# Making keys and values of four batches of the second cross-attention during the first experts' sorting

## The chip, the cores and the metric

One core of one Trainium2 chip runs the whole program. The metric is the device time of one execution in microseconds (us). Every operand is float32. The engines are TensorE (PE in the profile, with PEld for its weight loads), VectorE (DVE), ScalarE (ACT), GpSimd (POOL) and SyncE (SP), which here only issues transfers.

## The reference

A decoder of two layers on 16 sequences of 112 tokens of width 256, with a context of 16 x 375 x 256 that both layers read. Cut to what matters:

```
x = x + L0_attn(layernorm(x))                 # linear attention, 16 heads
x = x + L0_xattn(layernorm(x), ctx, ctx)      # softmax, 16 heads of 16
n = layernorm(x)
s = sigmoid(n @ gate_w + gate_b)              # 16 experts, the best two per token
x = x + n + shared_mlp(n) + sum(w_k * expert_k(n))
x = x + L1_attn(layernorm(x))                 # softmax, 16 heads of 64
x = x + L1_xattn(layernorm(x), ctx):          # softmax, 8 heads of 64
      cn = layernorm(ctx) * g2 + b2           # with a norm inside
      k, v = split(cn @ Wkv)                  # 256 -> 512 and 512
x = x + L1_ffn(layernorm(x))                  # 8 experts of width 1024, capacity 33 per sequence
```

K and V of the second cross-attention depend on the context and on weights alone, not on x.

## The kernel before, in words

The program keeps x in SBUF as 112 x 16 x 256 and works stage by stage. All large weights go through one SBUF tensor, `w_all`, of 3 x 6144 columns; `load_w` (line 155 on) loads a weight into a part of it through SP's queue.

The first cross-attention (from line 632, closures `scores`, `shifted`, `weights`, `values`) runs 16 batches of four quads of heads. The order of TensorE, VectorE, GpSimd and SP is written out by hand there. While batch b is worked on, K and V of batch b+1 are made (`prep_c`, `prep_k`, `prep_v`), spread over partitions by eight small transfers each (`kz<-kn`, `qz<-qn`), and the weights of expert b are loaded. `ctx_stats` takes mean and variance of each context for the later stage. After the loop come the last batch's division, transposes, projection, norm and router logits, and between them on TensorE the shared expert of the first expert stage in four groups of four batches: `shared_up` (line 765: eight PE instructions of 448 columns), `swiglu` (line 346: Silu on ScalarE, a product on VectorE), `shared_down` (line 774: eight PE instructions and two additions to x on VectorE).

The first expert stage (from line 888) orders only TensorE by hand; a scheduler orders the other engines by its own estimate of durations. It takes the sigmoid, the best two experts of each token (`top_two`, line 284), counts tokens before each by matmuls with `both` and `cnt`, and makes slot numbers `su` for both choices. 32 indirect transfers on GpSimd's queue (line 963, `xg<-xrow,su`) scatter the rows of x with two more columns (row number and weight, `xrow<-meta`, line 982) into the DRAM buffer `xg`, which was filled with zero rows early on (line 343). The rows are read back in 43 blocks of 128 (`fetch`, line 991, `xb<-xg`); every fetch waits for all scatters. The fetches run five blocks ahead through eight buffers:

```
for n in range(NB0 + 3):
    if n < NB0:
        fetch(n + 5)
        turn(n)          # two transposes (996), copy to bxT on VectorE (998)
    if 0 <= n - 1 < NB0:
        up(n - 1)        # four PE instructions with the block's expert
    if 0 <= n - 2 < NB0:
        turn_act(n - 2)
    if 0 <= n - 3:
        down(n - 3)      # own and to on VectorE (1025, 1026), scatter to yo
```

`own` and `to` are the target rows of a block's result, made from the columns of xb alone. The three W_qkv weights of the next stage (one MB each) are loaded ahead of the fetches.

The self-attention of the second layer (`pieces1`, `scores1`, `turned1`, `values1`) runs 32 units of one batch and half of the heads. Each unit takes three small pieces from a list `todo` that makes the following q, k and v; at the list's end stand `x1_first`, the pieces of the next stage for batch 0.

The second cross-attention (closures from line 1241) runs 32 units (b, u) of one batch and four heads. A unit issues the transposes of its softmax weights (line 1319), the scores of the next unit (1287), then fill work, then its values (1335). The fill work for batch b+1 is: `c_piece` (normalise the context, lines 234 and 1256, with scale and bias on ScalarE, 1259), four `k_piece` (1266 copies on ScalarE) and three `v_piece` (1273 copies on VectorE). When b+1 is a multiple of 4, four `q_piece` for the next four batches come in the first unit too. The softmax goes VectorE maximum (1298), ScalarE exponential (1299), VectorE reciprocal (1308), GpSimd division (1310). The second experts follow. A matmul in float32 shows as two PE instructions.

Of the kernel before, what the change touches and what calls it, by code (L numbers as in the profile page):

```python
# [18 lines left out]
S = 375  # L19
# [75 lines left out]
def tile_decoder(ctx: ExitStack, tc: tile.TileContext, t: dict, out: bass.AP):  # L95
# [238 lines left out]
    lg = f0.tile([L, B, E0], F32, tag="lg", name="lg")  # L334
    fill = f0.tile([128, RW], F32, tag="fill", name="fill")
    xg = dr.tile([NB0 * BLK, RW], F32, tag="xg", name="xg")
# [10 lines left out]
    def swiglu(sp, pg, pu, n):  # L347
# [3 lines left out]
        return sg  # L351

    cstack = ExitStack()
    cxp = pool(cstack, "cx", 2)
    cxs = {b: load_ctx(cxp, b) for b in range(2)}


# [284 lines left out]
    with ExitStack() as ph:  # L642
# [3 lines left out]
        def ctx_stats(b):  # L646
            cx = cxs.pop(b)
            for j in range(NKC):
                stats_of(cmv[:, b * NKC + j, :], cx[:, j, :])
            rstd_pow(cr[:, b * NKC : (b + 1) * NKC], cmv[:, b * NKC : (b + 1) * NKC, 1])  # L650
            if b + 2 < B:
                cxs[b + 2] = load_ctx(cxp, b + 2)


# [109 lines left out]

        def shared_up(g):
            pg, pu = bank(), bank()
            for i, p in enumerate((pg, pu)):
                mm_sum(
                    p[:, : 4 * L],
                    [(w_sh[:, i * 256 + c * 128 : i * 256 + (c + 1) * 128], xT(c, 4 * g, 4)) for c in range(2)],  # L770
                )
            return swiglu(lp, pg[:, : 4 * L], pu[:, : 4 * L], 4 * L)

        def shared_down(g, act):
            for j in range(2):
                po = bank()
                for i in range(2):
                    a = (2 * j + i) * L
                    mm(po[:L, i * D : (i + 1) * D], act[:, a : a + L], w_sh[:, 512:], start=True, stop=True)
                b = 4 * g + 2 * j  # L780
                xb = x[:, b : b + 2, :].rearrange("p b d -> p (b d)")
                nc.vector.tensor_add(xb, xb, po[:L, :])

        def out0(b):
# [11 lines left out]
        with tc.manual_schedule(engines={E.PE, E.DVE, E.Pool, E.SP}):  # L796
# [21 lines left out]
            for n, (b, g) in enumerate(quads):  # L818

                if b + 1 < B and g == 0:  # L820
                    prep_c(b + 1)
                    prep_q(b + 1)
                if b + 1 < B and g == 1:
                    prep_k(b + 1)
                if b + 1 < B and g == 2:
                    prep_v(b + 1)
                if g == 3:
                    load_expert(b)
                if g == 1 and b > 1:
                    norm_T(b - 2)  # L830
                if g == 3 and b + 2 < B:
                    norm_T(b + 2)
                if b:
                    if g == 2 and b > 1:
                        logits(b - 2)
                    if g == 1:
                        divide(b - 1)
                    if g == 2:
                        oT[b - 1] = out_T(b - 1)
                    if g == 3:  # L840
                        out_proj(b - 1, oT.pop(b - 1))
                qm = shifted(b, g)
                if n + 1 < len(quads):
                    scores(*quads[n + 1])

                if g == 0:
                    if b + 2 < B:
                        stats(b + 2)
                    if b > 1:
                        out_norm(b - 2)  # L850
                if g == 1 and b + 2 < B:
                    norm(b + 2)
                if g == 2 and b + 1 < B:
                    ctx_stats(b + 1)
                if g == 3 and b:
                    stats(b - 1)
                pr = weights(b, g, qm)
                if behind is not None:
                    values(*behind)
                behind = (b, g, pr)  # L860
            out_norm(B - 2)
            a0 = shared_up(0)
            values(*behind)
            norm_T(B - 2)
            a1 = shared_up(1)
            divide(B - 1)
            shared_down(0, a0)
            logits(B - 2)
            oT = out_T(B - 1)
            a2 = shared_up(2)  # L870
            out_proj(B - 1, oT)
            stats(B - 1)
            shared_down(1, a1)
            out_norm(B - 1)
            norm_T(B - 1)
            shared_down(2, a2)
            logits(B - 1)
            a3 = shared_up(3)
            shared_down(3, a3)

    e0s.close()
    cstack.close()
    with tc.issue_after(kz_loaded[B - 1]):
        w_qkv = load_w(2 * WR, [t["L1_attn_W_qkv"][i] for i in range(3)])

# [4 lines left out]
    with ExitStack() as ph:  # L890
        lp = pool(ph, "f0", 2)
        l1 = pool(ph, "f0one", 1)
        one = lambda shape, name: l1.tile(shape, F32, tag=name, name=name)
        with tc.manual_schedule(engines={mybir.EngineType.PE}):
            lgf = lg.rearrange("p b n -> p (b n)")
# [6 lines left out]
            both = one([L, B * E0], "both")  # L902
            nc.vector.tensor_add(both, flat(oh0), flat(oh1))

            pc = bank()
            for i in range(2):
                mm(pc[:, i * L : (i + 1) * L], both[:, i * 128 : (i + 1) * 128], ones[:L, :L], start=True, stop=True)
            cnt = one([128, 2, L], "cnt")
            nc.vector.tensor_copy(cnt.rearrange("p i l -> p (i l)"), pc[:, : 2 * L])
            pr = bank()  # L910
            later = const("later").rearrange("p (i n) -> p i n", i=2)
# [4 lines left out]
            pn = bank()  # L916
            mm_sum(pn[:L, :E0], [(cnt[:, i, :], const("same")) for i in range(2)])

            nt = one([L, E0, NT // BLK], "nt")
# [15 lines left out]
            for k, o in enumerate((oh0, oh1)):  # L935
# [4 lines left out]
                slots.append(su)  # L940

            tot = one([L, B], "tot")
            meta = one([L, 2, B, 2], "meta")
            nc.vector.tensor_add(tot, v0, v1)
            nc.vector.reciprocal(tot, tot)
            nc.vector.tensor_copy(meta[:, :, :, 0], const("row_id", L).rearrange("p (k b) -> p k b", k=2))
            for k, v in enumerate((v0, v1)):
                nc.vector.tensor_mul(meta[:, k, :, 1], v, tot)

# [29 lines left out]

            for k in range(2):  # L980
                for g in range(4):
                    nc.vector.tensor_copy(xrow[:, 4 * g : 4 * g + 4, D:], meta[:, k, 4 * g : 4 * g + 4, :])
                    for b in range(4 * g, 4 * g + 4):
                        scatter("xg", xg, slots[k][:, b : b + 1], xrow[:, b, :])

            xbs, xTs, cols, acts, aTs = {}, {}, {}, {}, {}

            def fetch(j):
                if j < NB0:
                    xbs[j] = lp.tile([BLK, RW], F32, tag="xb", name="xb", bufs=8)  # L990
                    after_all("xg", nc.sync.dma_start(xbs[j], xg[j * BLK : (j + 1) * BLK, :]))

# [23 lines left out]
            def down(j):  # L1016
# [10 lines left out]
                scatter("yo", yo, to[:, 0:1], os_[:, :])  # L1027

            for j in range(5):
                fetch(j)  # L1030
            for n in range(NB0 + 3):
# [7 lines left out]
                if 0 <= n - 3:  # L1039
                    down(n - 3)  # L1040
    f0s.close()
    cxp = pool(cstack, "cx", 2)
# [90 lines left out]
    with ExitStack() as ph:  # L1133
# [108 lines left out]

        def fetch(b):
            if b < B:
                cxs[b] = load_ctx(cxp, b)

        def c_piece(b, c):
            if c == 0:
                fetch(b + 2)
                for j in range(NKC):  # L1250
# [103 lines left out]
        def combine(b):  # L1354
# [8 lines left out]
        x1_first = (  # L1363
            [lambda c=c: c_piece(0, c) for c in range(2)]
            + [lambda m=m: q_piece(0, m) for m in range(4)]
            + [lambda m=m: k_piece(0, m) for m in range(4)]
            + [lambda j=j: v_piece(0, j) for j in range(3)]
        )
        with tc.manual_schedule(engines={mybir.EngineType.PE}):
# [51 lines left out]
            for n, (b, u) in enumerate(units):  # L1421
                pT = turned(pr)
                pr = scores(*units[n + 1]) if n + 1 < len(units) else None
                if u == 0:
                    nc.gpsimd.tensor_add(x[:, b, :], x[:, b, :], bout)
                if b + 1 < B:
                    if u == 0:
                        c_piece(b + 1, 0)
                        c_piece(b + 1, 1)
                if late:  # L1430
# [5 lines left out]
                if u == 0 and b:  # L1436
                    project(oT2.pop(b - 1), wo, 4, b - 1, keep=(mv1, r1))
                if b + 1 < B:
                    if u == 0:
                        if (b + 1) % 4 == 0:  # L1440
                            q_piece((b + 1) // 4, 0)
                            q_piece((b + 1) // 4, 1)
                        k_piece(b + 1, 0)
                        k_piece(b + 1, 1)
                        if (b + 1) % 4 == 0:
                            q_piece((b + 1) // 4, 2)
                            q_piece((b + 1) // 4, 3)
                        v_piece(b + 1, 0)
# [139 lines left out]
```

## Time and profile before

| What | us |
|---|---|
| median of 3 runs | 1801.3 (1796.4 to 1809.83) |
| the profiled execution | 1802.55 |
| its span, first to last instruction | 1800.8 |
| TensorE busy | 1607.3 (89%) |
| VectorE, ScalarE, GpSimd busy | 973.5, 604.5, 518.3 |
| chain that ended last, TensorE's share | 55% |
| last matmul of the routing ends | 503.2 |
| first transposes of an expert block | 551.72 |
| first scores of the second cross-attention | 985.59 |
| last unit's transposes of that stage end | 1358.6 |

The times of single instructions come from the timeline of the profiled execution, counted from the span's start. In such a row stand start, duration, engine, line and operation, output and inputs, shape and count, and in brackets how long the engine had been idle and what released it. L116 is the helper that all matmul sums go through, so there the tile names tell the work. In the rows of the slices each digit is a tenth of a slice of 45 us.

### The profile page before, as it was taken

To read this page: it belongs to the slowest core of one execution; us is meant where nothing else is said; L and a number is where in the kernel's file an instruction comes from. 1 tells how busy PE (TensorE), PEld (TensorE's weight loads), DVE (VectorE), ACT (ScalarE), POOL (GpSimd) and SP (SyncE) were. 2 spreads that over 40 slices of the span, in tenths; PEclk is the share of its full clock that TensorE was granted. 3 is DMA by queue.
4 is the path that set the end of the run, shared out by engine and by line. 5 is a ranking of instruction groups with operands and counts; after the bars stand their busy time and mean duration, and the time that the engine had idled before them with its cause. 6 is when DMAs were issued, how large, how long until landed. Compare 5 with 4: busy or idle time off the path is not lost.

```text
span 1800.8 us, 30940 instructions
## 1 busy us (share of the span) xinstructions
PE 1607.3 (89%) x11755; PEld 1207.5 (67%) x11755; DVE 973.5 (54%) x2635; ACT 604.5 (34%) x1456; POOL 518.3 (29%) x685
## 2 busy tenths in 40 slices
PE   7889999999806968999999999999997999979992
PEld 5766666666504746788786566666665888858881
DVE  7976777777623437777665545655456222232222
ACT  3433444444302522233323333444341333313330
POOL 6641221211153523333332444434441000030003
PEclk9999999999958979999999999999997999989996
DMA  6402222222224451000000100000001444454422
GB/s 173 107 9 52 59 72 65 60 64 56 71 80 124 145 194 52 2 1 1 1 1 9 41 18 18 19 12 19 15 16 33 146 137 147 160 158 153 152 83 67
DMA packets 96077, 125.57 MB, mean 70 GB/s; under 512 B 14353, under 2 KB 81082, under 8 KB 95930
## 3 DMA queue, kind: packets, MB, share of 16 engines
q1 hardware_dynamic: 88042, 107.98, 19.8%
q0 software_dynamic: 5184, 13.13, 2.3%
q10 hardware_dynamic: 2704, 2.49, 0.5%
q8 instruction: 94, 1.54, 0.4%
q14 instruction: 53, 0.43, 0.1%
HBM read 94.40 MB, written 21.18 MB: 64 GB/s over the span
## 4 chain that ended last, share of the span: by engine, by line
PE 55%; DMA 3%; DVE 3%; POOL 2%; issue 1%; ACT 1%; POOLq 0%; ACTq 0%; DVEq 0%; SPq 0%
PE pT L116 41%; PE pT L1319 3%; PE pT L1287 2%; PE pT L1335 2%; DMA got<-eo,row 2%; PE pT L1194 1%; PE pT L1229 1%; PE pT L1215 1%; PE pT L1120 1%; DMA yb<-yo 1%; POOL pr L1310 1%; PE pT L1514 1%; PE pT L263 1%; PE pT L1256 1%; DVE x_res L1359 0%
## 5 line engine op out<-in xcount | busy, mean ns | idle before, releaser
L1310 POOL TENSOR_SCALAR pr<-pr,den 112x375 f32<-112x375 f32 x128 | 155.9, 1236 | 197.0 <-DVE den L1308 197.0
L1490 DVE SCALAR_TENSOR_TENSOR hT<-pT,vT,gt 128x264 f32<-128x264 f32 x128 | 62.9, 492 | 241.8 <-ACT gt L1489 241.7
L116 PE MATMUL pT<-xnT,w_all 128*128 128x224 f32 (+2 forms) x736 | 161.6, 371 | 0.5 <-DVE xnT L265 0.5
L116 PEld LDWEIGHTS pT<-xnT,w_all 128*128 128x128 f32 x736 | 132.5, 195 | 17.5 <-issue 13.9
L1527 POOL DMA_INDIRECT got<-eo,row x32 | 30.1, 942 | 394.0 <-DVE hT L1490 215.6
L712 ACT ACTIVATE pr<-pT 125x336 f32<-125x336 f32 x256 | 94.6, 456 | 133.8 <-PE pT L703 133.8
L116 PE MATMUL pT<-w_all 128*128 128x264 f32 (+1 forms) x576 | 136.7, 394 | 0.6 <-ACT w_all L596 0.6
L116 PE MATMUL pT<-cT,w_all 128*128 128x375 f32 x384 | 134.3, 489 | 0.2 <-ACT cT L1259 0.2
L116 PE MATMUL pT<-w_all,cT 128*125 128x256 f32 (+1 forms) x384 | 133.3, 490 | 0.0
L687 DVE TENSOR_REDUCE mx<-pT 112x1 f32<-112x375 f32 x256 | 122.1, 539 | 11.9 <-PE pT L685 10.5
L116 PE MATMUL pT<-hT,w_all 128*128 128x264 f32 x512 | 119.4, 392 | 6.6 <-ACT hT L1495 6.6
L116 PEld LDWEIGHTS pT<-w_all 128*128 128x128 f32 (+1 forms) x576 | 110.3, 193 | 20.3 <-ACT w_all L596 0.8
L116 PE MATMUL pT<-e1T,w_all 128*128 128x264 f32 x512 | 118.4, 390 | 0.0
L1207 POOL TENSOR_TENSOR pr<-pr,den 112x448 f32<-112x448 f32 x64 | 59.2, 946 | 200.6 <-DVE den L1205 149.4
L116 PEld LDWEIGHTS pT<-hT,w_all 128*128 128x128 f32 x512 | 99.0, 194 | 24.4 <-ACT hT L1495 7.0
L116 PEld LDWEIGHTS pT<-e1T,w_all 128*128 128x128 f32 x512 | 97.9, 193 | 16.7
L116 PE MATMUL pT<-w_all,oT 128*112 128x256 f32 x448 | 106.4, 383 | 0.1
L116 PEld LDWEIGHTS pT<-cT,w_all 128*128 128x128 f32 x384 | 71.5, 192 | 52.2 <-issue 10.1
L116 PE MATMUL pT<-w_all,xnT 128*112 128x256 f32 (+1 forms) x320 | 104.7, 475 | 1.8 <-DMA w_all<-in_L_attn_Wv_dram 0.9
L1489 ACT ACTIVATE gt<-pT,vT 128x264 f32<-128x264 f32 x128 | 61.3, 480 | 114.6 <-PE pT L116 91.1
L116 PEld LDWEIGHTS pT<-w_all,cT 128*125 128x125 f32 x384 | 69.5, 187 | 43.6 <-issue 31.5
L1144 ACT COPY pT<-pT 112x448 f32<-112x448 f32 (+1 forms) x64 | 34.1, 532 | 168.0 <-PE pT L1319 90.2
(248 smaller groups left out, 2986.9 us busy)
## 6 DMA issues: line engine op xcount, KB each, us to landing
w_all<-in_L_ffn_w_c_fc_dram SPq DMA_DIRECT2D x16, 1024.0 KB
w_all<-in_L_ffn_w_gate_dram SPq DMA_DIRECT2D x16, 1024.0 KB
w_all<-in_L_ffn_w_c_proj_dram SPq DMA_DIRECT2D x16, 1024.0 KB
cx<-in_ctx_dram SPq DMA_DIRECT2D x32, 375.0 KB
kz<-kn SPq DMA_DIRECT2D x128, 46.9 KB
xg<-fill SPq DMA_DIRECT2D x1, 5547.0 KB
xb<-xg SPq DMA_DIRECT2D x43, 129.0 KB
eo<-os SPq DMA_DIRECT2D x16, 264.0 KB
```

Source lines behind the costliest of these rows:

```text
L116: mm(o, l, r, start=(i == 0), stop=(i == len(terms) - 1))
L687: nc.vector.tensor_reduce(mx[b % 2][:, g, i, 16:17], ps[i][:L, :S], AX.X, ALU.max, negate=True)
L712: nc.scalar.activation(pr[:, i, :], pw[i][:KC, : NKC * L], AF.Exp)
L1144: nc.scalar.copy(dst, src)
L1207: nc.gpsimd.tensor_tensor(pr[:, k], pr[:, k], bcast(den[:, k, :], L), ALU.mult)
L1287: mm(ps[2 * s + k][:L, :S], qTs[b // 4][rows(k), m, (b % 4) * L : (b % 4 + 1) * L], kTs[b][rows(k), m, :], start=True, stop=True,)
L1310: nc.gpsimd.tensor_scalar(pr[:, n, :], pr[:, n, :], den[:, n : n + 1], None, ALU.mult)
L1319: nc.tensor.transpose(pt[:KC, (n % 4) * L : (n % 4 + 1) * L], pr[:, i, j * KC : (j + 1) * KC], ident[:L, :L])
L1335: mm(po[rows(k), s * L : (s + 1) * L], vs[b][:, j, h * 64 : (h + 1) * 64], pT[:, 3 * (2 * s + k) + j, :], start=(j == 0), stop=(j == NKC - 1),
L1489: nc.scalar.activation(gt, ps[1][:, :HS], AF.Identity, bias=vec(n_v + e * NJ + j), scale=1.0)
L1490: nc.vector.scalar_tensor_tensor(hT[:, j, :], ps[0][:, :HS], vec(12 + e * NJ + j), gt, ALU.add, ALU.mult)
L1527: nc.gpsimd.indirect_dma_start(out=got[:, :], out_offset=None, in_=eo[b // HB][:, :], in_offset=bass.IndirectOffsetOnAxis(ap=row[k][:, b : ...
```

## The change

- `AHEAD = (0, 4, 8, 12)`: for these batches the contexts are loaded once more at the end of the first cross-attention (`ctx_ahead`), normalised on VectorE (`norm_ahead`), transposed and scaled (`c_ahead`), and K and V are made (`k_ahead`, `v_ahead`, copied by ScalarE). Each K and each V is stored to DRAM (`kd`, `vd`, 0.77 MB each) from ScalarE's queue. These are 36 pieces in a list `ahead`: for each batch two c, four k, three v. `take(n)` issues the next n on TensorE: seven in the tail of the first cross-attention, eight before the count of tokens, one inside it, 13 after the first 16 scatters are issued, seven at the end.
- The shared expert moves from that tail to beside the last 16 scatters: group g-1 after the scatters of group g.
- The scheduler no longer orders VectorE between the sigmoid and the end of `take(7)`: that part is in the order of the program. The blocks' VectorE work (bxT, own, to) stays with the scheduler. The row number and weight columns (`told`) and the first slots `su` come in another order.
- Wkv of the second cross-attention is loaded a first time in batch 2 of the first cross-attention. The three W_qkv loads move from ahead of the fetches to behind fetches 12, 17 and 22.
- In the second cross-attention no c, k and v pieces are made for batches 0, 4, 8, 12; `k_load` and `v_load` bring them from DRAM on SP's queue. The four q pieces are spread two and two over the pair of units.
- The zero rows for `xg` are copied from a part of `w_all` in place of a tile of their own.

```diff
+    def norm_ahead(i):
+        for j in range(NKC):
+            n = AHEAD[i] * NKC + j
+            normed(acxs[i][:, j, :], acxs[i][:, j, :], cmv[:, n, 0:1], cr[:, n : n + 1])
...
+    def k_ahead(i, m):
...
+        pk = bank()
+        mm_sum(pk[:, :S], [(wkv_a[0][:, c, m * 128 : (m + 1) * 128], acTs[i][:, c, :]) for c in range(2)])
+        nc.scalar.copy(akv[i][:, m, :], pk[:, :S])
+        if m == 3:
+            nc.scalar.dma_start(kd[AHEAD[i]], akv[i])
...
+                if (b, g) == (2, 0):
+                    wkv_a += load_w(2 * WR, [t["L1_xattn_Wkv"]])
...
+                if b == B - 1 and g in (1, 2):
+                    norm_ahead(g - 1)
...
             out_norm(B - 2)
-            a0 = shared_up(0)
+            take(3)
             values(*behind)
             norm_T(B - 2)
-            a1 = shared_up(1)
+            take(1)
             divide(B - 1)
-            shared_down(0, a0)
             logits(B - 2)
+            take(1)
             oT = out_T(B - 1)
-            a2 = shared_up(2)
+            take(1)
             out_proj(B - 1, oT)
             stats(B - 1)
-            shared_down(1, a1)
+            take(1)
             out_norm(B - 1)
             norm_T(B - 1)
-            shared_down(2, a2)
             logits(B - 1)
-            a3 = shared_up(3)
-            shared_down(3, a3)
...
-        with tc.manual_schedule(engines={mybir.EngineType.PE}):
+        with tc.manual_schedule(engines={mybir.EngineType.PE, mybir.EngineType.DVE}):
...
+            take(8)
...
+            norm_ahead(2)
...
+            take(1)
...
+            norm_ahead(3)
+            for g in range(4):
+                told(0, g)
...
+            for g in range(4):
+                rows_to(0, g)
+            take(len(ahead) - 7)
+            for g in range(4):
+                told(1, g)
+                rows_to(1, g)
+                if g:
+                    shared(g - 1)
+            shared(3)
+            take(7)
+
+        with tc.manual_schedule(engines={mybir.EngineType.PE}):
...
+                    i = (j - 12) // 5
+                    if j in (12, 17, 22):
+                        with tc.issue_after(got.ins):
+                            w_qkv.extend(load_w(2 * WR + 2048 * i, [t["L1_attn_W_qkv"][i]]))
...
+        def k_load(b):
+            kTs[b] = lp.tile([128, 4, S], F32, tag="qk", name="kt")
+            nc.sync.dma_start(kTs[b], kd[b])
...
-            [lambda c=c: c_piece(0, c) for c in range(2)]
-            + [lambda m=m: q_piece(0, m) for m in range(4)]
-            + [lambda m=m: k_piece(0, m) for m in range(4)]
-            + [lambda j=j: v_piece(0, j) for j in range(3)]
+            [lambda m=m: q_piece(0, m) for m in range(4)]
+            + [lambda: k_load(0), lambda: v_load(0)]
...
+                if b + 1 in AHEAD and u == 0:
+                    k_load(b + 1)
+                    v_load(b + 1)
```

## What was predicted

> **What bounds the kernel now.** I read the busy slices first, then the windows around the hole that they show, then the timelines of that hole and of the second cross-attention.
>
> ```profile
> ## 2 busy tenths in 40 slices
> PE   7889999999806968999999999999997999979992
> POOL 6641221211153523333332444434441000030003
> PEclk9999999999958979999999999999997999989996
> 500.00:520.00 20.00, 3.19 (x11) 2.25 (x9) 6.40 (x19) 0.00 (x0) 9.34 (x10) 0.59 0.17 51
> 520.00:540.00 20.00, 0.00 (x0) 0.00 (x0) 0.34 (x2) 0.00 (x0) 15.13 (x17) 0.50 0.30 93
> ```
>
> A slice is 45 us. TensorE is nearly full everywhere but in slice 11 (495 to 540 us). The windows (columns: PE, PEld, DVE, ACT, POOL busy, granted clock, DMA share, GB/s) say who works there: only GpSimd, and the clock is at half.
>
> ```profile
> 500.72 2.47 PE L116 MATMUL pT<-call,cnt 128*112 128x256 f32 x8
> 551.72 1.19 PE L996 MATMUL pT<-call,xb 128*128 128x128 f32 x4 [48.54 <-DMA xb<-xg]
> 507.92 1.20 POOL L963 DMA_INDIRECT xg<-xrow,su  x1 [23.10 <-DVE su L939]
> 546.80 0.94 POOL L963 DMA_INDIRECT xg<-xrow,su  x1 [0.30 <-issue]
> 549.52 3.66 SPq L991 DMA_DIRECT2D xb<-xg  x8
> 553.71 0.15 DVE L1025 TENSOR_SCALAR own<-xb 128x1 f32<-128x1 f32 x1 [0.27 <-DMA xb<-xg]
> ```
>
> 32 scatters at 1.247 us each (507.92 to 547.7) hold TensorE for 48.5 us; the blocks' rows xb come only after the last. Elsewhere TensorE is the bound:
>
> ```profile
> 1064.60 1.52 PE L1287 MATMUL pT<-kt,qt 64*112 64x375 f32 x8
> 1071.87 2.69 PE L116 MATMUL pT<-cT,w_all 128*128 128x375 f32 x8
> 1077.40 1.88 PE L116 MATMUL pT<-w_all,cT 128*125 128x512 f32 x4
> 1349.93 1.52 PE L1287 MATMUL pT<-kt,qt 64*112 64x375 f32 x8
> 1357.99 0.58 PE L1319 MATMUL pT<-call,pr 112*125 112x112 f32 x3 [0.63 <-POOL pr L1310]
> ```
>
> 1064 is a unit (four heads of one batch) with K and V of the next batch in it; no wait is marked. 1349.93 is the last unit, with nothing to fill it: from its scores to the end of its transposes it takes 1357.99 + 0.58 - 1349.93 = 8.64 us, however little TensorE does, because the softmax passes through VectorE, ScalarE and four GpSimd divisions of 1236 ns. That is the floor of a unit.
>
> **Second cross-attention, batches 4, 8, 12: gain.** The pair of units before such a batch (its K, V and the four q pieces in it) takes 1064.60 to 1092.56 = 27.96 us. From the PE timeline, by starts: its first unit is 17.40 us, less context transposes 0.69, K 2.53, V 1.81, and two of four q pieces 3.00 = 9.37. The second is 10.55, less V 3.45 and K 2.62, plus the two q pieces 3.00 = 7.48, so the floor of 8.64 holds. Pair after: 18.0; gain 9.95, times three = **29.9 us**. Of the 11.1 us of work removed per pair 1.15 goes to the floor. K and V come back by two loads of 0.77 MB on SP's queue. They may start once the buffers of batch b-2 are free, a whole pair (over 22 us) before the scores that need them; at the 124 GB/s of the first xb fetches and contexts before (1.8 MB between 549.52 and 563.9) both take 12.7 us. Cost 0, covered by that pair; behind them on SP wait only context loads of later batches.
>
> **End of the self-attention, batch 0: gain.** There 11 us of context, K and V pieces sit among the last three units (957.66 to 984.67). Rebuilt with what stays: values at 962.4, last scores 963.3, two transposes and the last q piece until 967.5. The softmax of the last scores took 8.5 us in the unit before (955.68 to 964.14, where the transposes after GpSimd start), so TensorE waits until 971 to 972, then transposes, out-projection 3.5, values 0.9: first cross scores at 976.7 instead of 985.59, gain 8.9. The 3.4 us wait may drop the clock; up to 3 us, I charge 1. **7.9 us.**
>
> **From the end of the first cross-attention to the expert blocks: loss.** Order of instructions in the built kernel, costed by rows:
> - VectorE normalises two contexts inside the last batch: 6 at 0.41 us, between the maxima and the next query, on the chain there: 1.8 us later.
> - The shared expert's 20.5 us of matmuls (four times 3.2 and 1.9) leave the tail; seven small pieces (1.3 to 1.8 us each) take their place. Chain of the last batch (divide, transposes, projection, statistics, norm, logits) rebuilt row by row: last logits at 483.9 instead of 486.7; sigmoid 2.6; 12 routing operations at 0.455 without the 3.5 us that VectorE spent waiting for the shared expert: `both` at 492.1 against 498.76. Eight more pieces (10 us) keep TensorE until 493.7; the three routing products then run at full clock with one V piece (1.8) between; slots 3.5 us after them; first scatter 502.0 against 507.9. Normalising contexts 8 and 12 (2.4 us) lies beside these matmuls.
> - Scatters are 32 as before: first xb load at 502.0 + 41.6 = **543.6** against 549.5.
> - TensorE meanwhile: 13 pieces 16.1 us, shared expert groups 6.4 us each; up-matmuls of group 3 end near 536. And there it stops: in VectorE's stream the scheduler put own and to of blocks 0 to 3 ahead of group 3's gate product. They wait for rows fetched after all scatters: 553.71 + 0.15 - 549.52 = 4.4 us after the first fetch, so 548.0. Queued behind on VectorE: that product, the additions to x, the next contexts, the first bxT; behind these on TensorE: group 3's down-matmuls (1.9) and the seven pieces of batch 12 (K 5.35, V 5.45). So 12.7 us meant for the hole come after it.
> - The idle 12 us drop the clock. Here rule and trace differ. Rows: after 551.72 the clock is 0.50 to 555, 0.56 to 558, then 1.00: six us of half speed; after the wait at 642, 0.50 and 0.56 again for six us of steady work. The Trainium skill ("TensorE: Matmul & The Clock Gate", What's actually happening) gives about 3.4 us of sustained work. By it the restart costs 1.7 us, by the rows 3.0; I take 3.0.
> - Blocks start at 548.7 + 12.7 + 3.0 = 564.4; the transposes of block 5 seven us later (a block takes 1.63 us), 571.4, against 565.72 in the timeline of before (which lost time there to the contexts of the next stage, 560.8 to 565; these now land behind the 12.7 us). **Loss 5.7 us.** If that cover went, the contexts, 14.4 us after the first fetch, would hold the first bxT until 559, and the front would gain only about 0.3.
>
> Another rule speaks against this part: "SBUF — State Buffer" (SBUF: two separate sides) says that some VectorE operations lock GpSimd out of its port, so that it cannot write the descriptors of its DMAs. Now VectorE works beside scatters. Rows: the 43 scatters beside a busy VectorE (yo) average 959 ns, the 32 with it idle 949. By the rule the scatters could lose up to VectorE's 9 us of shared-expert work (0.62 + 2 x 0.69 per group), by the row 32 x 0.01 = 0.3 us. I take 0.
>
> **Transfers moved.** Eight stores of 0.77 MB go from ScalarE's queue; issue rows of SP are 0.3 to 0.6 us, so some 4 us of ScalarE, half idle there: 0. The cross Wkv load (1 MB) passes SP's queue in batch 2 of the first cross-attention, ahead of kz and qz: 4 us at 257 GB/s (495 to 498), beside a lead of two quads; 0 to 3, I take 0.5. The three W_qkv loads (1 MB) move from before the scatters to between xb fetches 12 and 23. Each is 4 us ahead of the next xb on SP's queue; fetches run five blocks of 1.63 us = 8.2 us ahead and land in 2.6: 6.6, so just hidden: 0, up to 4 us each exposed. The fill rows' source moves into the weight area: 0.
>
> **Sum.** 29.9 + 7.9 - 5.7 - 0.5 = 31.6 us. Span 1800.8 - 31.6 = 1769.2. Around the span lie 1.75 us (the profiled execution is 1802.55), so 1770.9 for such a run; the median of the runs, 1801.3, is 1.25 below it: 1769.7, **1770 us**.
>
> **Rivals.**
> 1. *VectorE's queue does not hold group 3* (fetches early or pieces done): the front then gains 0.3 instead of losing 5.7: **1764**. Against it: the order of the instructions is fixed in the build, and 21.89 us of waiting at own<-xb already stand in the trace of before. 0.12.
> 2. *The expert blocks starve.* W_qkv, the last K and V stores and xb share the engines; three times 4 us exposed: **1782**. For it: 6.6 of 8.2 us is thin, share 0.45 already. Against: 382 to 400 GB/s at 651 to 663 show headroom. 0.19.
> 3. *The reloads take the place of the matmuls.* If K and V of batches 4, 8, 12 were fetched only when asked for, six transfers of 6.3 us = 38 us stand open and eat the gain: 1770 + 38 = **1808**. It decides for slower than before once over 31.6 us are exposed, five of six loads in full. Against: DMA share 0.04 in that stage and buffers free a pair ahead. 0.04.
> 4. *The clock or the floor cost more* (pairs at 9.5 per unit, cold restarts at both places): 3 x 1 + 2 + 3 = 8 us, **1778**; inside the likeliest case's spread.
>
> **How the numbers follow.** Likeliest 0.65 with 1762 to 1778 as its own range. Rival 1 takes the low end to 1757 (its spread below 1764), rival 2 the high end to 1784. About 1 per cent, 18 us, is what a measurement of this kernel tells from no change: below 1783.3 lie the likeliest, rival 1 and more than half of rival 2: 0.87; within 1 per cent 0.09; slower 0.04.
>
> **What would show it.** Right: a TensorE wait of about 12 us near 536 to 548 before the shared down-matmuls, released through VectorE's gate product or own; K and V matmuls just after it at half clock; first xb fetch near 543; pairs before batches 4, 8, 12 near 18 us with about 1 us of waiting on GpSimd per second unit; first cross scores 1 to 3 us earlier than 985.6 in absolute time (7.9 gained, 5.7 and 0.5 lost). Wrong: no such wait (rival 1), turns waiting on xb around blocks 13 to 23 (rival 2), scores waiting on kt (rival 3), or scatters clearly above 1.25 us apart.

## The result, and the profile after

| What | before | after |
|---|---|---|
| median of 5 runs, us | 1801.37 (1796.4 to 1809.83) | 1787.13 (1785.51 to 1789.56) |
| ratio, 95% interval | | 0.9918 (0.9889 to 0.9947) |
| profiled execution / its span | 1802.55 / 1800.8 | 1788.28 / 1786.5 |

The change gains 14 us where 31.6 were forecast, and the time lies above the range. A second measurement of the changed kernel, taken beside the experiments, gave 1793.39 (1789.81 to 1797.74) against 1803.31: ratio 0.9944 (0.9926 to 0.9962).

The slices of the changed kernel, then the rows that answer to those shown of before:

```profile
## 2 busy tenths in 40 slices
PE   7889999999896777999999799999997999979992
POOL 5632111222152341333332345454441000030003
PEclk9989999999998898999999899999997999989996
```

The hole of slice 11 (digit 0 before) is filled, but slices 13 to 15, the expert blocks, read 777 where 968 stood, and slice 22, where the second cross-attention begins, 7 for 9. These two places are what the forecast missed.

```profile
504.41 1.21 POOL L1050 DMA_INDIRECT xg<-xrow,su  x1 [18.08 <-PE pT L116]
...
546.16 3.67 SPq L1088 DMA_DIRECT2D xb<-xg  x8
...
548.25 0.15 DVE L1127 TENSOR_SCALAR own<-xb 128x1 f32<-128x1 f32 x1 [13.48 <-DMA xb<-xg]
...
550.92 3.75 PE L962 MATMUL pT<-w_all,sg 128*112 128x256 f32 x8 [13.87 <-DVE own L1127]
```

This is the hold that the prediction described: the down-matmuls of group 3 wait 13.87 us through VectorE's own, then run at half clock (3.75 us for what takes 1.98 warm).

A pair of units with its batch made early, by the starts of the scores:

```profile
1081.08 1.52 PE L1401 MATMUL pT<-kt,qt 64*112 64x375 f32 x8
1090.64 1.52 PE L1401 MATMUL pT<-kt,qt 64*112 64x375 f32 x8
1099.32 1.52 PE L1401 MATMUL pT<-kt,qt 64*112 64x375 f32 x8
```

1099.32 - 1081.08 = 18.24 us, where 27.96 stood (the other two such pairs take 18.66 and 18.23).

Where the time came from and went, from matching TensorE instructions of the two traces (minus is a gain):

| Stretch | before, us | after, us | difference |
|---|---|---|---|
| start to the first cross-attention, 131 us | | | +5.7 |
| from there to the transposes of block 5 | at 565.72 | at 573.75 | +2.3 |
| transposes of block 5 to the end of the last down-matmul | 72.2 | 86.7 | +14.5 |
| to the first self-attention product | 13.0 | 13.1 | +0.1 |
| self-attention, to the first cross scores | 334.7 | 323.8 | -10.9 |
| first unit of the cross-attention | 8.65 | 13.42 | +4.8 |
| pairs before batches 4, 8, 12 | 84.4 | 55.1 | -29.3 |
| other units | 271.3 | 271.7 | +0.4 |
| second experts, to the last product | 417.0 | 414.9 | -2.1 |
| sum | | | -14.5 |

The first row is not put down to the change. Up to 131 us TensorE's order is the same in both kernels, and the first transposes of that stage (at 132.57 us before, 138.29 after) come 1.0 to 5.1 us later than 132.57 in the eleven profiles of the next section, the kernel before with the loads alone (1.1) among them. In the second profile of the changed kernel they come 1.8 us late. The same sum for that second profile is -11.5 us; there the front (second row) costs 10.8 instead of 2.3 us and the expert blocks (third row) 11.8 instead of 14.5.

### The profile page after: what moved, and what is told of

It reads as the page before. It is cut to its first block, busy times and chain, and to the rows that moved or that the text cites. A ratio compares the mean times of both kernels' runs of the same rounds, so it can differ in the third digit from the quotient of the medians.

```text
span 1786.5 us, 30980 instructions
## 1 busy us (share of the span) xinstructions
PE 1614.7 (90%) x11755; PEld 1212.9 (68%) x11755; DVE 965.2 (54%) x2623; ACT 609.2 (34%) x1466; POOL 518.5 (29%) x685
## 5 line engine op out<-in xcount | busy, mean ns | idle before, releaser
L116 PE MATMUL pT<-w_all 128*128 128x264 f32 (+3 forms) x632 | 157.1, 403 | 1.4 <-ACT w_all L388 0.8
L116 PEld LDWEIGHTS pT<-w_all 128*128 128x128 f32 (+2 forms) x632 | 119.3, 191 | 28.7 <-issue 3.9
L116 PE MATMUL pT<-cT,w_all 128*128 128x375 f32 x320 | 112.9, 492 | 0.4 <-ACT cT L1373 0.4
L116 PE MATMUL pT<-w_all,cT 128*125 128x256 f32 (+1 forms) x336 | 111.5, 476 | 0.0
L1413 ACT ACTIVATE pr<-pT,top 112x375 f32<-112x375 f32 x128 | 72.4, 572 | 55.7 <-DVE top L1412 53.3
L116 PEld LDWEIGHTS pT<-w_all,oT 128*112 128x112 f32 x448 | 78.4, 183 | 16.5 <-issue 0.4
```

Of the source, the lines that this page charges most:

```text
L116: mm(o, l, r, start=(i == 0), stop=(i == len(terms) - 1))
L1413: nc.scalar.activation(pr[:, i, :], ps[i][:L, :S], AF.Exp, bias=top[:, i : i + 1], scale=1.0, accum_out=den[:, i : i + 1],)
```

## The experiments

Times of kernels in this section stand beside runs of the kernel before on the same chip. "Block 5 to last down" is the third row of the table.

**The loads alone, in the kernel before.**

```diff
-    with tc.issue_after(kz_loaded[B - 1]):
-        w_qkv = load_w(2 * WR, [t["L1_attn_W_qkv"][i] for i in range(3)])
...
+                    if j in (12, 17, 22):
+                        with tc.issue_after(got.ins):
+                            w_qkv.extend(load_w(2 * WR + 2048 * i, [t["L1_attn_W_qkv"][i]]))
```

> The kernel before with one part of the change alone: the three W_qkv loads (1 MB each) leave the place ahead of the scatters and go behind the fetches of blocks 12, 17 and 22. Theory (the loads delay the yo scatters, whose four-deep buffers stop VectorE's queue): from the transposes of block 5 to the last down-matmul 83 to 87 us instead of 72, TensorE's waits on sg about 13 us instead of 3.4, time 10 to 14 us above the kernel before, 1811 to 1815. Rival A (the loss of the expert stage comes from the late, cold start behind own<-xb): 72 us as before, time within 2 us of 1801. Rival B (xb arrives late): the same time as the theory, but the waits stand at the block transposes on xb.

Measured: 1817.16 against 1804.37, ratio 1.0077 (1.005 to 1.0104), 13 us slower. Block 5 to last down 84.8 us; TensorE's waits on sg 12.9. The front is that of the kernel before here (first block transposes at 552.65), with none of the change's hold or late start, and 12.6 us of loss are in the stage all the same, so rival A falls. The waits stand on sg and not on xb, so rival B falls as well.

How one load does it, in windows of the changed kernel around the first (columns: PE, PEld, DVE, ACT, POOL busy, clock, DMA share, GB/s), then the timeline:

```profile
582.00:585.00 3.00, 3.00 (x18) 2.38 (x16) 0.93 (x4) 1.78 (x6) 1.66 (x3) 1.00 0.74 200
585.00:588.00 3.00, 0.19 (x1) 0.00 (x0) 0.00 (x0) 0.28 (x1) 0.85 (x1) 0.96 1.01 390
588.00:591.00 3.00, 1.83 (x6) 1.54 (x7) 1.21 (x8) 0.73 (x2) 0.00 (x0) 0.50 0.07 26
591.00:594.00 3.00, 3.00 (x10) 2.25 (x10) 0.92 (x4) 0.81 (x4) 0.96 (x1) 0.50 0.28 88
```

```profile
588.57 0.16 DVE L1128 TENSOR_TENSOR to<-own,xb 128x1 uint32<-128x1 f32 x1 [5.42 <-DMA yo<-os,to]
...
588.84 0.28 DVE L350 TENSOR_TENSOR sg<-sg,pT 128x128 f32<-128x128 f32 x1
589.03 0.42 DVE L1100 COPY bxT<-pT 128x256 f32<-128x256 f32 x1
...
589.17 0.48 PE L1114 MATMUL pT<-call,sg 128*128 128x128 f32 x1 [3.98 <-DVE sg L350]
```

The load takes all 16 DMA engines for 3 us. The three yo scatters in flight (issued at 581.64, 583.26 and 584.89) land after 6.9, 6.0 and 5.0 us, where the median of all 43 is 2.4. The instruction to, which must not overwrite the row numbers that the first of them still reads, waits 5.42 us for its landing at 588.55. The gate product sg and the copy bxT, whose inputs are ready, stand behind it on VectorE. TensorE stops for 3.98 us, and its clock stands at half in the next two windows. The totals over the stage, before and then after (us in total, times, longest):

```profile
DVE to L1026 <- DMA yo<-os,to: 29.5, 32, 2.9
...
PE pT L1012 <- DVE sg L350: 3.4, 5, 1.5
```

```profile
DVE to L1128 <- DMA yo<-os,to: 35.9, 25, 5.4
...
PE pT L1114 <- DVE sg L350: 13.5, 7, 4.0
```

VectorE waited for scatters before, too: 29.5 us in waits of up to 2.9, which TensorE hardly felt. The loads made a few of these waits longer than the slack that VectorE had.

**Deeper buffers.**

```diff
-                os_ = lp.tile([BLK, D], F32, tag="os", name="os", bufs=4)
+                os_ = lp.tile([BLK, D], F32, tag="os", name="os", bufs=7)
...  (to and own the same)
```

> The changed kernel with os, to and own seven deep instead of four; the W_qkv loads stay where they are. Theory: VectorE may run three blocks (4.9 us) further ahead of the scatters, about the excess of the longest waits over those of before (5.4 against 2.9), so most of the stall goes: block 5 to last down 74 to 78 us instead of 86.7, time 1775 to 1780. Rival B (bandwidth or late xb): no change, 1787. Rival A (cold start): no change, 1787.

Measured: 1791.7, ratio 0.9939 (0.992 to 0.9959); block 5 to last down 84.2 us. A miss: no gain against the changed kernel (84.0 in its second profile). The reason stands in the order of VectorE's instructions, given below: with three more buffers the scheduler moved to three blocks forward, so that it waited for the very same scatter.

**The loads cut into twelve.**

```diff
-                    if j in (12, 17, 22):
+                    if 0 <= i < 3 and k % 2 == 0:
...
+                            nc.sync.dma_start(w_qkv[i][:, :, 128 * k : 128 * k + 256], rows_of(t["L1_attn_W_qkv"][i])[:, :, 128 * k : 128 * k + 256])
```

> The changed kernel with each W_qkv load cut into four of 256 KB, one behind every second fetch from block 12 to 34; same bytes, buffers four deep. Theory (a single 1 MB load holds the DMA engines for some 3 us): each piece delays a scatter by under 1 us, block 5 to last down 73 to 77 us, time 1774 to 1779. Rival B (the bytes themselves are the cost): 84 to 87 us, 1785 to 1788. Rival A: 1787.

Measured: 1784.58, ratio 0.9892 (0.9873 to 0.9912); block 5 to last down 75.6 us. The same bytes in smaller pieces cost 3.4 us over the kernel before, instead of 11.8 in one piece each (second profile): the sum of the bytes is not what counts. The pieces also lie over more blocks (12 to 34 instead of 12 to 22), so the length of one transfer and its spacing are not told apart here.

**No loads.**

```diff
-                            w_qkv.extend(load_w(2 * WR + 2048 * i, [t["L1_attn_W_qkv"][i]]))
+                            pass
```

> The changed kernel without any W_qkv load: the self-attention reads the bytes of the cross-attention's K and V weights in their place, so that part of the computation is changed and the rest is as it was. Theory: block 5 to last down 72 to 74 us as before, time 1773 to 1776; the gap of this to the changed kernel is what the three loads cost. Rival A (cold start or the reordered VectorE queue): 84 to 87 us stay, time 1787.

Measured: 1781.38, ratio 0.9878 (0.9858 to 0.9898); block 5 to last down 72.6 us, as before the change.

**The changed kernel again,** without an edit.

> The changed kernel itself beside the others on this chip. In the three runs of its variants (deeper buffers, cut loads, no loads) TensorE's second shared-expert products finished some 17 us after they were issued, with no other engine to wait for, and the last four scatters came 10 us late; the profile of the changed kernel does not show this. Theory: it belongs to the chip or the run and shows here too, with the first block transposes at 570 to 575 us instead of 565.9 and a time of 1788 to 1795. Rival: it belongs to the edits; then 565.9 and 1787 again.

Measured: 1793.39, ratio 0.9944 (0.9926 to 0.9962); first block transposes at 570.45. So what held these profiles up between 516 and 540 us does not come from the edits (more of it in the last section); block 5 to last down 84.0 us. The times expected of the cut loads and of no loads were counted from 1787 and came out over 5 us too low; against 1793.39 the two are 8.8 and 12.0 us faster.

**VectorE in program order.**

```diff
-        with tc.manual_schedule(engines={mybir.EngineType.PE}):
+        with tc.manual_schedule(engines={mybir.EngineType.PE, mybir.EngineType.DVE}):
...
+                    with tc.issue_after(last_to[0]): normed(cxs[b][:, j, :], cxs[b][:, j, :], cmv[:, n, 0:1], cr[:, n : n + 1])
```

(`last_to` is the last block's to.)

> The changed kernel with VectorE's stream of the expert blocks in program order (own and to of blocks 0 to 3 no longer ahead of group 3's gate product) and the next contexts normalised after the last block's to. Theory (the hold at own<-xb leaves the shared expert's last group and batch 12's pieces after the scatters, at half clock): no wait before the down-matmuls of group 3, the pieces run beside the last scatters, first block transposes about 15 us earlier than in the changed kernel run here, time 12 to 16 us below it. Rival (TensorE then waits for the rows xb instead, and the blocks start when they did): under 3 us.

Measured: 1769.24 (1767.92 to 1774.77), ratio 0.9815 (0.9788 to 0.9842), 24 us below the changed kernel. The size was out at both places. The front gains only 4.3 us (first block transposes 566.17 against 570.45), 0.6 of it from the start of the run. The wait before group 3's down-matmuls shrinks from 2.61 to 0.78 us as meant, but the hold-up at 516 us, which stands in both kernels, had already taken most of the time that was to be gained. But block 5 to last down falls to **65.2 us**, below the 72 of the kernel before, with the one-MB loads in place. Windows of this kernel over two of them:

```profile
591.00:594.00 3.00, 3.00 (x18) 2.52 (x18) 1.44 (x7) 1.41 (x6) 1.68 (x2) 1.00 1.00 378
...
600.00:603.00 3.00, 3.00 (x18) 2.52 (x17) 1.69 (x8) 1.78 (x6) 1.86 (x2) 1.00 1.01 375
```

DMA share 1.00 and 375 GB/s, about as in the changed kernel, and TensorE busy 3.00 of 3 us. The transfers are as heavy, but to does not wait for a scatter once in this trace (26 times in the second profile of the changed kernel), so nothing that TensorE needs stands behind such a wait. My own account had the lead of the buffers in it and not the place of to in the queue.

**Program order and cut loads.** The edits of both.

> The program-order version with the W_qkv loads cut into twelve of 256 KB, one behind every second fetch from block 12. If the two costs add: the gain of the program-order version and that of the cut loads (block 5 to last down 73 to 77 us instead of 86), together 23 to 28 us below the changed kernel, 1759 to 1765. If the program order alone already hides the late scatters: no better than the program-order version by more than 4 us.

Measured: 1770.55, ratio 0.9808 (0.9781 to 0.9835); block 5 to last down 65.0 us. Nothing is added: with to out of the way the loads cost nothing in one piece either.

**To early again.**

```diff
-                to = lp.tile([BLK, 1], U32, tag="to", name="to", bufs=4)
...
+                    with tc.issue_after(last_to[0]): mark(n)
+                    turn(n)
```

Here `mark(n)` makes own and to of block n, and `last_to` keeps it behind the shared expert's last addition to x.

> The program-order version with one thing turned back: own and to of block n stand in VectorE's stream ahead of bxT of block n and the gate product of block n-1 (as the scheduler had put them), instead of behind those of three blocks later. They do not stand ahead of the shared expert's group 3, so the hold stays away. Theory (to of block n needs the scatter of block n-4, issued about one block before, and what stands behind it on VectorE is what TensorE needs): block 5 to last down 80 to 88 us instead of 65, time 14 to 22 us above the program-order version, 1783 to 1791. Rival (the W_qkv loads matter by themselves, or the program order gained by the contexts moved away): 65 to 68 us, time within 4 us of 1769.

Measured: 1833.57, ratio 1.0158 (1.0131 to 1.0184); block 5 to last down 126.7 us. The direction holds and decides between the theories; the size is about three times the most that I expected (64 us above the program-order version), since the wait returns with nearly every block (waits between 578 and 700 us, in total, times, longest):

```profile
DVE to L1129 <- DMA yo<-os,to: 85.9, 36, 7.1
...
PE pT L116 <- DVE bxT L1100: 45.0, 25, 4.9
```

The five orders side by side, read from VectorE's timeline in mid-stage. To of block k needs the scatter of block k-4 (k-7 with seven buffers), whose down-matmul TensorE issues in turn k-1 (k-4):

| Kernel | ahead of bxT of block 16 stands | needs the scatter of | lead in blocks | block 5 to last down, us |
|---|---|---|---|---|
| before | to 14 | 10 | 3 | 72.2 |
| after | to 14 | 10 | 3 | 86.7, 84.0 |
| deeper buffers | to 17 | 10 | 3 | 84.2 |
| program order | to 12 | 8 | 5 | 65.2 |
| to early | to 16 | 12 | 1 | 126.7 |

The lead orders the times, and where it is 3, the loads make the difference.

**Three batches.**

```diff
-    AHEAD = (0, 4, 8, 12)
+    AHEAD = (4, 8, 12)
```

(Batch 0's c, k and v pieces are back in `x1_first`.)

> The changed kernel with three batches made early (4, 8, 12); batch 0's contexts, K and V stay at the end of the self-attention as before the change. By the prediction's terms: loses the 7.9 us at the end of the self-attention. By the trace of the changed kernel: loses 10.9 us there and takes back the 4.8 us by which the first unit of the cross-attention grew (its layer-norm chain is covered again, 8.7 us instead of 13.4), net 6 us slower than the changed kernel in that place; the front changes by less than 3 us, since the pieces fall into the time of the scatters. 1788 to 1795 in all. Rival (those pieces cost the front as much as they give at the self-attention): no slower than the changed kernel.

Measured: 1791.18, ratio 0.9932 (0.9908 to 0.9957), not slower. Self-attention to first scores 334.3 us (before 334.7, changed kernel 324.8 in its second profile), first unit 8.90 us: both as expected. But the first block transposes come 7.9 us earlier (562.52 against 570.45), which I had at under 3. By the time alone the rival is right: batch 0's pieces give nothing in all. The traces qualify it: the last scatter is 6.1 of these 7.9 us earlier (542.95 against 549.09), because the gap that the hold-up leaves before the last four is 5.0 us here and 10.6 in the changed kernel. Whether fewer pieces made the hold-up shorter or this run had less of it is open.

**The first unit.**

```diff
-            flush(0)
+            q_piece(0, 2); q_piece(0, 3); c_piece(1, 0); c_piece(1, 1); k_piece(1, 0); k_piece(1, 1); flush(0)
```

(The same pieces are taken out of their old places.)

> The program-order version with the last two q pieces and the context and first two K pieces of batch 1 between the first cross scores and their transposes. Theory (the layer-norm chain of batches 14 and 15, uncovered since batch 0's pieces left, costs the first unit 4.8 us): what was idle is filled, first two units together 3 to 5 us shorter, time 1764 to 1767. Rival (VectorE itself is late, whatever TensorE does): the work only changes places, under 1 us.

Measured: 1766.28, ratio 0.9803 (0.9783 to 0.9823), the best here; the intervals of this kernel and the program-order version overlap, so their difference of 3 us is not settled by the times. In the traces the first two units take 27.5 us together instead of 30.0, 2.5 less where 3 to 5 were expected. The first unit stays long (13.9); its TensorE wait is filled:

```profile
977.42 1.52 PE L1401 MATMUL pT<-kt,qt 64*112 64x375 f32 x8
978.87 3.27 PE L116 MATMUL pT<-xnT,w_all 128*128 128x448 f32 x8
...
983.64 2.79 PE L116 MATMUL pT<-cT,w_all 128*128 128x375 f32 x8 [0.86 <-ACT cT L1373]
...
991.32 1.52 PE L1401 MATMUL pT<-kt,qt 64*112 64x375 f32 x8
```

In the changed kernel the same unit, with the layer-norm chain of the last batches in it:

```profile
997.30 1.52 PE L1401 MATMUL pT<-kt,qt 64*112 64x375 f32 x8
1003.80 0.61 PE L263 MATMUL pT<-call,xn 112*128 112x112 f32 x2 [4.97 <-DVE den L1422]
```

**Stores on another queue.**

```diff
-            nc.scalar.dma_start(kd[AHEAD[i]], akv[i])
+            (nc.sync if i < 3 else nc.scalar).dma_start(kd[AHEAD[i]], akv[i])
```

> The program-order version with the six K and V stores of batches 0, 4 and 8 on SP's queue instead of ScalarE's. Asked: whether the 17 us by which the second shared-expert products finish late beside the scatters come from those stores on ScalarE's queue. If so: those products finish 2 us after their start, first block transposes at about 553 to 556 instead of 566, time 1757 to 1760. If not: 1769 again, the last four scatters 10 us late again.

Measured: 1770.86, ratio 0.9817 (0.98 to 0.9835); first block transposes at 567.29. The hold-up is there unchanged; it does not come from these stores on ScalarE's queue.

## Why the prediction was wrong, point by point

**Wrong, and the main miss: "Transfers moved", the three W_qkv loads, "6.6, so just hidden: 0".** Measured 11.4 to 14.5 us, shown from three sides: the loads alone in the kernel before cost 12.6 us in the stage (84.8 less 72.2), leaving them out gives 11.4 back (84.0 to 72.6), cutting them 8.4. The first profile's 14.5 is 2 to 3 us more than any of these, and no other run shows that part. The step asked whether the xb fetches run far enough ahead and found that 6.6 of 8.2 us are needed. They do: no block transpose waited for xb. It did not ask what else was in flight on the same DMA engines. The yo scatters were, and the trace of before shows VectorE waiting for them 32 times, up to 2.9 us; that was the tight lead, not xb's. The Trainium skill ("DMA: Bandwidth & Descriptors", Queues, rings and completion order) says that each DMA engine goes round between the queues that it has work for, a packet at a time; the share of 1.01 and the wait of 5.42 us agree with a scatter that shares its engines with a load. Rival 2 had the size (12 us) with the wrong wait; its sign in the profile, "turns waiting on xb", did not come.

**Not forecast: the first unit, 4.8 us.** "End of the self-attention, batch 0" was put at 7.9; the stage gained 10.9, and the first unit of the next lost 4.8, 6.1 together. The pieces taken out had also covered the layer-norm chain of the last batches. The step rebuilt TensorE up to the first scores and stopped there. With batch 0's pieces put back the unit takes 8.90 us.

**Right in the first profile, and partly by luck: the front.** There the hold through own (13.87 us), the pieces at half clock and their place came as described. The first xb load came at 546.16, 2.6 later than forecast with 5.7 us of a late start in it, and up to block 5 the front lost 2.3 us where 5.7 were charged. The second profile shows another picture: the first scatter came at 500.35 (forecast 502.0), but TensorE then waited 18.87 us before the down-matmuls of group 1, the first xb load came at 551.95, group 3 waited only 2.61 us, and the front lost 10.8 us. The step knew nothing of that hold-up (last section). The clock followed the rows: in the first profile 0.50 until 555 and 0.66 from 555 to 558, so six us of half speed from 550.92 on, and not the 3.4 that the prediction set against them. Rival 1, no hold at all, is what the program-order version makes; it brought the front 4.3 us in runs with the hold-up.

**Right: the pairs,** 29.3 us for 29.9, 18.2 to 18.7 each for 18.0; no scores waited for kt or vt (rival 3 falls). **Right: Wkv** in the first cross-attention, no loss found for 0.5. The stores on ScalarE's queue and the lock between VectorE and GpSimd cost nothing that the traces show: in the first profile the 31 scatters after the first follow each other at (543.31 - 504.41) / 31 = 1.255 us, before at (546.80 - 507.92) / 31 = 1.254. The page that the prediction names for this lock speaks of some VectorE operations; that the shared expert's products and additions are among them was the prediction's own assumption, and no run shows it. The working also has two slips that move nothing: that VectorE work is 4 x 2.0 = 8.0 us and not 9, and two loads of 0.77 MB at 124 GB/s take 12.4 us and not 12.7.

By the table the change gave 14.5 us, 17.1 less than forecast. The expert blocks are 14.5 of these, the self-attention with the first unit 1.8, the pairs 0.6, the start of the run 5.7; the front and Wkv cost 3.9 less than the 6.2 charged, and the stretches without a forecast gave 1.6 (2.1 less 0.5), for which the traces were not searched. Of the 14.5, 11.4 to 12.6 are shown to be the loads. That the start is the run's is argued from its spread of 1.0 to 5.1 us over the later profiles, not shown.

## What to carry to other kernels

Before a large load is put beside small transfers, look for the shortest lead among all that wait for a transfer in that stretch, not only for what comes behind the load on its own queue. An instruction that waits for a transfer belongs in its engine's stream behind everything that the bound engine needs next; more buffers do not help if a scheduler spends them on moving the wait forward. Work taken off the bound engine uncovers the chain that it had hidden: rebuild the stage through the first unit behind it.

## What the runs showed of the hardware

In the first profile of the changed kernel the shared expert's products beside the scatters finish as issued. In ten of the eleven later profiles they finish late; the eleventh is the kernel before with the loads alone, where TensorE has no such work. VectorE and TensorE in the second profile of the changed kernel:

```profile
516.65 1.98 PE L962 MATMUL pT<-w_all,sg 128*112 128x256 f32 x8 [2.66 <-DVE sg L350]
518.47 3.17 PE L116 MATMUL pT<-xnT,w_all 128*128 128x448 f32 x8
540.51 3.75 PE L962 MATMUL pT<-w_all,sg 128*112 128x256 f32 x8 [18.87 <-DVE sg L350]
```

```profile
522.23 0.69 DVE L965 TENSOR_TENSOR x_res<-x_res,pT 112x512 f32<-112x512 f32 x1 [5.64 <-PE pT L116]
529.93 0.69 DVE L965 TENSOR_TENSOR x_res<-x_res,pT 112x512 f32<-112x512 f32 x1 [7.01 <-remote]
...
539.84 0.62 DVE L350 TENSOR_TENSOR sg<-sg,pT 128x448 f32<-128x448 f32 x1 [9.13 <-remote]
```

Products issued by 518.5 were seen by VectorE at 522.2 and 529.9, those issued by 521.6 at 537.6 (ScalarE) and 539.8. The steps between are 7.7 us in several kernels. For it the last four scatters come some 4 to 10 us late, and in the second profile the stretch from the routing products to the first blocks is 75.8 us instead of 67.2. It came with one program both ways, on two chips, with and without the W_qkv loads, and with the stores on either queue. "Remote" means that the profile shows no instruction that ended the wait. The ends of TensorE's products are modelled, so the rows do not tell whether the products or their signals were late. A load of instructions is not it, as far as recorded: the second profile has none on its DMA queues between 511.2 and 553 us. The cause stays open. It may be why the second measurement of the changed kernel (1793.39) lies above the first. The variants of the changed kernel all show it and are compared with that second measurement, or within a stretch that lies behind it.
